# A four-layer graph stack on one core: the first feed-forward product as seven block products with streamed weights

## The chip, the cores and the metric

The kernel runs on one core of a Trainium2 chip, in one launch. The core has five engines with an instruction queue each: TensorE (PE in the profile, its weight loads PEld), VectorE (DVE), ScalarE (ACT), GpSimd (POOL) and SyncE (SP, which here issues every DMA). All data are 32-bit floats. The metric is the device time of a launch in microseconds (us); lower is better.

## The reference, cut to what matters

Four layers run one after the other over 128 graphs of 64 nodes with 512 features. Each adds its result to its input and normalizes the sum. Layer 0 is a linear neighbour sum, layer 1 a graph attention with four heads, an output attention and a feed-forward part, and layers 2 and 3 are plain graph attentions. The feed-forward part of layer 1 is what the change is about:

```python
h = jax.nn.elu(_gat_heads(enc_inputs, adj, W_heads, a_heads))
h = jnp.transpose(h, (0, 2, 1, 3)).reshape(B, N, -1)
out = _gat_heads(h, adj, W_out[None], a_out[None])[:, 0]
out = jax.nn.elu(out)
ffn = jnp.maximum(out @ w1 + b1, 0.0) @ w2 + b2
y = ffn + out
```

Here `w1` and `w2` are 512 x 512, and `out` has 512 features for each node.

## The kernel before, in words

**Tiling.** The 8192 nodes are cut into 32 pairs of tiles, T = 2 tiles of P = 128 nodes each. Every pair goes through stages, each a Python generator: `stage_first` (layer 0), `stage_scores` (the heads' attention), `stage_heads`, `stage_project` (the product with W_out), `stage_out` (output attention, feed-forward, norm) and `stage_gat` for layers 2 and 3. Several pairs are under way at once, in different stages. The last pair takes another way from the output attention on: `stage_last` loads whole weights, and `stage_tile` does each of its two tiles by itself with plain products.

**Seven products.** A product of two matrices, each cut into 2 x 2 blocks, can be had from seven block products instead of eight, with additional sums of blocks before and after (the Strassen-Winograd form). `seven` (L633) is the frame for this: it takes two PSUM tiles, `stx_...` and `sty_...`, issues product 0 to 6 with a pause of `gap` between them, and adds the results into the four blocks of the output. With `fresh` the first write of a block is a copy on ScalarE (four of them), and three adds on VectorE follow. `once` is the hook for a subtraction that must come after the first product, `whole` the hook for what follows when half of the output is ready. No more than UNITS = 3 such units are under way together.

There are two uses of it. `strassen` (L685) keeps the tokens stationary and moves the weights: a block product has `kc` matmuls with 256 moving columns. It serves layer 0, W_out, w2, W2 and W3. The heads (L1007) keep the weights stationary and move the tokens, so that their result comes out transposed: a block product is 2 x 2 matmuls with 128 moving columns.

**Weights.** `stage_stream` (L580) runs once for each streamed weight near the start: it loads the four blocks, stores three of them to DRAM as they are, forms four differences on GpSimd and stores these too. `part_from` (L613) later loads one of the seven parts for one product. For weights of 512 rows a part is 256 KB and lies in the ring `wk` of six buffers, which w2, W2 and W3 share; the ring `ws` of four buffers is for parts of 512 KB.

**The first feed-forward product**, in `stage_out` (L1112 to L1127), is not of this kind. `w1` is loaded once (L562) and stays on chip, 8 KB on each partition. For each pair it makes the tile `hid`, transposed, from the transposed input `oT`: two PSUM tiles `hidp`, each with two groups of four matmuls of 256 moving columns, and a Relu with the bias on ScalarE out of PSUM for each group. `oT` and `hid`, like the tiles `gT` of layers 2 and 3, are of the tag "A", of which there are NA = 2 buffers. After `hid` come its sums and the product with w2, whose tiles are named `y_...`.

**Order.** No instruction is issued where it is written. The class `Plan` records every operation as a step with a rank, its place in the recording, and `order` (L229) then simulates the five queues with a rough cost for each step (`cost`, L353) and issues on each engine what is ready with the lowest rank. `WAIT` and `SLACK` are the delays that it supposes between engines, `NEAR` is how far a step may run ahead for a free buffer, and the table `LATER` shifts the rank of steps by kind: "te:hidp/S" stands for TensorE steps that write hidp in the first 11% of all steps, "/E" for those in the last 7%. All DMAs are issued by SP in the order that comes out of this, and each waits there for its buffer. In the profile nearly everything has the line L336, where steps are played, so that tiles are told apart by name.

Of the kernel before, what the change touches and what calls it, by code (L numbers as in the profile page):

```python
# [12 lines left out]
FP = mybir.dt.float32  # L13
BF = mybir.dt.bfloat16
I32 = mybir.dt.int32
AF = mybir.ActivationFunctionType
# [21 lines left out]

WAIT = 0.152
NEAR = 150
SLACK = {"tensor": 0.8, "sync": 0.4}

LATER = {
    "gp:never/S": -100, "gp:rs_i": -60, "gp:s_o/S": -20, "gp:ys/E": -40, "sc:aT": -100,
    "sc:aTg/S": 20, "sc:elu/S": -40, "sc:hT": 120, "sc:oT": 60, "sc:who": -80, "sc:xT": -200,  # L50
    "sc:xT/S": -180, "sc:ys/S": 132, "sy:beta/S": -12, "sy:raw_w": 180, "te:fp/S": -20,
    "te:hidp/E": -40, "te:hidp/S": 28, "te:l": 29, "te:l/S": 69, "te:pt": -28, "te:pt/E": 200,
    "ve:e": -29, "ve:e/S": 40, "ve:f_o/S": -120, "ve:hT": 100, "ve:has": 200, "ve:mv": -100,
    "ve:mv/E": 100, "ve:mx": -20, "ve:o": -140, "ve:r": -40, "ve:r/E": 40, "ve:sh": 10,
    "ve:sm": -80, "ve:st": -13,
}


# [315 lines left out]
def gnn_stack_kernel(  # L374
# [45 lines left out]
        nc.sync.dma_start(out=t, in_=x[ts(p, T * P), :].rearrange("(t p) d -> p t d", p=P))  # L420
        return t

    def weight(src, rows, name):
        t = wp.tile([P, rows // P, D], FP, tag=name, name=name)
        nc.sync.dma_start(out=t, in_=src.rearrange("(c p) o -> p c o", p=P))
        return t
# [282 lines left out]
    def sums(A, kc, eng):  # L709


        def make(name):
            s2, s3 = (
                unit.tile([P, kc, P], FP, tag=f"s{i}", bufs=2, name=f"s{i}_{name}")
                for i in (2, 3)
            )
            eng.tensor_tensor(s2, A(0, 1), A(0, 0), ALU.subtract)
            eng.tensor_tensor(s3, A(1, 1), s2, ALU.subtract)
            return (
                A(0, 1), s2, s3,  # L720
                lambda a: eng.tensor_tensor(a, a, s2, ALU.subtract),
            )
        return make


    def moments(x, name):
# [280 lines left out]
    def stage_heads():  # L1007

        for i in range(NP * H):
            p, h = divmod(i, H)  # L1010
            while p not in ys:
                yield 1.0
            y, t1, t2 = ys[p][h // 2]
            y, t1, t2 = y[:, :, h % 2, :, :], t1[:, :, h % 2, :], t2[:, :, h % 2, :]
            Y = lambda k, t: y[:, 2 * k : 2 * k + 2, t, :]
            w = w_h[h]
            hT = unit.tile([P, KC, T, P], FP, tag="hT", bufs=H, name=f"hT_{p}_{h}")

            def product(i, ps, first, last):
                a = w[:, :, (2, 0, 1, 4, 6, 5, 3)[i], :]  # L1020
                b = (Y(1, 0), Y(0, 0), t1, t2, Y(1, 1), Y(0, 1), Y(1, 0))[i]
                with nc.together():
                    for c in range(2):
                        for k in range(2):
                            nc.tensor.matmul(
                                ps[:, c, :], lhsT=a[:, k, ts(c, P)], rhs=b[:, k, :],
                                start=(first and c == 0 and k == 0),
                                stop=(last and c == 1 and k == 1), skip_group_check=True,
                            )

            def t4():
                nc.gpsimd.tensor_tensor(Y(1, 0), Y(1, 0), t2, ALU.subtract)

            yield from seven(
                product, lambda i, j: hT[:, 2 * i : 2 * i + 2, j, :], [2, P], f"h_{p}_{h}",
                TURN / H / 8 * haste(p), True,
                t4,
                lambda i: elu_of(hT[:, 2 * i : 2 * i + 2, :, :], f"{p}_{h}_{i}"),
            )
            hTs[p, h] = hT  # L1040
            if h == H - 1:
                ys.pop(p)
# [41 lines left out]
    def stage_out(p):  # L1084
# [19 lines left out]
        for t in range(T):  # L1104
            ps = psum.tile([P, KC, P], FP, tag="b", name=f"oTp_{p}_{t}")
            with nc.together():
                for k in range(KC):
                    nc.tensor.transpose(ps[:, k, :], o[:, t, ts(k, P)], ident)
            nc.scalar.copy(oT[:, :, ts(t, P)], ps)
            nc.gpsimd.tensor_tensor(o[:, t, :], o[:, t, :], b2_sb, ALU.add)  # L1110
            yield 2.0
        hid = unit.tile([P, 2, T, KC // 2, P], FP, tag="A", bufs=NA, name=f"hid_{p}")  # L1112
        for q in range(KC // 2):
            ps = psum.tile([P, 2, T * P], FP, tag="b", name=f"hidp_{p}_{q}")
            for c in range(2):
                with nc.together():
                    for k in range(KC):
                        nc.tensor.matmul(
                            ps[:, c, :], lhsT=w1_sb[:, k, ts(2 * q + c, P)], rhs=oT[:, k, :],
                            start=(k == 0), stop=(k == KC - 1),  # L1120
                        )
            for c in range(2):
# [69 lines left out]
    def stage_last(p):  # L1192

        raw = {}
        for name, src, tag, bufs in (("w2", w2, "ax", 1), ("W2", W2, "ys", 2), ("W3", W3, "ys", 2)):
            raw[name] = unit.tile([P, KC, D], FP, tag=tag, bufs=bufs, name=f"{name}_last")
            nc.sync.dma_start(out=raw[name], in_=src.rearrange("(c p) o -> p c o", p=P))
        r = unit.tile([P, 2, D], FP, tag="hT", bufs=H, name="rows_last")
        for i, src in enumerate((b2, gamma)):
            nc.sync.dma_start(out=r[:, i, :], in_=src.partition_broadcast(P))  # L1200
        who, aT = yield from out_attention(p)
        o = xp.tile([P, T, D], FP, tag="x", name=f"o_{p}")
        shared.update(raw=raw, rows=r, who=who, aT=aT, o=o)
        yield 2.0
        for name in ("2", "3"):
            shared[name] = rows([score[name][s, :] for s in range(2)], f"{name}_{p}")
            yield 2.0

    def stage_tile(p, t):
# [33 lines left out]
        for c in range(KC):  # L1243
            with nc.together():
                for k in range(KC):
                    nc.tensor.matmul(
                        ps[:, c, :], lhsT=w1_sb[:, k, ts(c, P)], rhs=oT[:, k, :],
                        start=(k == 0), stop=(k == KC - 1),
                    )
        for c in range(KC):  # L1250
# [52 lines left out]
    def start(at, order, stage):  # L1303
        heapq.heappush(queue, (at, order, stage))
# [88 lines left out]
```

## Time and profile before

| what | value |
|---|---|
| time, median of 3 runs | 3308.72 us (3306.71 to 3319.2) |
| the profiled execution | 3313.95 us |
| its span on the core | 3312.2 us |
| mean granted TensorE clock | 0.994 of full speed |
| matmul records of hidp in 31 pairs | 992, of 256 columns |
| matmul records of hidp in the last pair | 64, of 128 columns |
| DMA traffic | 726.08 MB, mean 219 GB/s |
| DMA instructions issued by SP | 2086 |

The span runs from the first to the last instruction of the program, and the launch around it makes up the rest of the execution's time. In a row of a group the columns are line, engine, operation, output<-inputs, shape and count, then busy time in us and mean ns of one, then the idle time before them and what ended it. The mean ns of one matmul is longer than its share of the engine, since matmuls overlap. Records whose operands differ have rows of their own.

First and last weight-stationary run of the hidden layer in stage_out: the first starts at 197.7 us, the last at 3205.9.

### The profile page before, as it was taken

The page shows a single profiled execution, that of the slowest core. Times are in us where ns is not written, and L with a number is a line of the kernel's source. Part 1 is how long each engine was busy: PE and PEld are TensorE (multiplying, and loading weights), DVE is VectorE, ACT ScalarE, POOL GpSimd, SP SyncE. Part 2 cuts the span into 40 slices and gives each one's busy share as a digit, 9 for nine tenths or more (in the row PEclk, how much of TensorE's full clock was granted, in tenths as well). Part 3 has the DMA queues.
Part 4 walks back from the last instruction along what each step waited for, and adds up shares of the span by engine and source line. Part 5 has one row for each costly group of instructions (what it writes and reads, how often), then busy time and mean ns, then how long its engine had stood idle before and what let it go on. Part 6 is the DMA issues. An engine that isn't in the chain of part 4 may idle for free.

```text
span 3312.2 us, 60000 instructions
## 1 busy us (share of the span) xinstructions
PE 3265.2 (99%) x21268; PEld 2881.8 (87%) x21268; DVE 2374.4 (72%) x5668; ACT 1364.6 (41%) x3226; POOL 1724.0 (52%) x1860
## 2 busy tenths in 40 slices
PE   8999999999999999999999999999999999999997
PEld 4888888898988989989889988888889899898885
DVE  5467767777777777777777777777777767777766
ACT  2434344343444434444443443434444344343442
POOL 6745445554555555455454555645554455554442
PEclk9999999999999999999999999999999999999998
DMA  8956666767667676667766667676666766667652
GB/s 303 338 177 215 221 203 215 234 208 237 211 210 233 213 247 197 200 230 221 242 204 220 212 217 236 214 226 208 214 233 208 246 201 202 229 216 238 227 183 77
DMA packets 306584, 726.08 MB, mean 219 GB/s; under 512 B 34240, under 2 KB 43504, under 8 KB 306288
## 3 DMA queue, kind: packets, MB, share of 16 engines
q1 hardware_dynamic: 306288, 722.26, 67.1%
q8 instruction: 171, 2.80, 0.3%
q14 instruction: 125, 1.02, 0.1%
HBM read 688.69 MB, written 33.44 MB: 218 GB/s over the span
## 4 chain that ended last, share of the span: by engine, by line
PE 91%; DVE 4%; DMA 3%; POOL 1%; issue 1%; ACT 0%; SPq 0%; POOLq 0%; DVEq 0%; ACTq 0%
PE stx_h L336 13%; PE stx_o L336 13%; PE stx L336 12%; PE sty_h L336 10%; PE sty_o L336 9%; PE sty L336 9%; PE hidp L336 7%; PE yp L336 4%; PE gp L336 3%; PE stx_y L336 3%; PE sty_y L336 2%; PE axp L336 2%; PE l L336 1%; PE op L336 1%; PE oTp L336 1%; DMA d_f<-f 1%
## 5 line engine op out<-in xcount | busy, mean ns | idle before, releaser
L336 DVE CUSTOM_DVE_ANT_0 j<-x,rows 128x512 bf16<-128x512 f32 x736 | 584.1, 794 | 94.3 <-DMA rows<-d_h 75.6
L336 PE MATMUL stx_h<-ys,wh 128*128 128x128 f32 x3072 | 403.8, 275 | 0.7 <-DVE hT L336 0.7
L336 PEld LDWEIGHTS stx_h<-ys,wh 128*128 128x128 f32 x3072 | 381.1, 192 | 22.3 <-DVE sh L336 5.7
L336 POOL TENSOR_SCALAR rs<-mv 128x1 f32<-128x1 f32 x256 | 104.1, 407 | 406.2 <-DVE mv L336 392.2
L336 ACT COPY hT<-stx_h 128x256 f32<-128x256 f32 x384 | 143.0, 372 | 384.6 <-PE stx_h L336 378.6
L336 ACT ACTIVATE x<-x,sh,rs 128x512 f32<-128x512 f32 x256 | 207.2, 813 | 223.6 <-DVE sh L336 221.0
L336 PE MATMUL sty_h<-ys,wh 128*128 128x128 f32 x2048 | 273.8, 277 | 0.0
L336 PEld LDWEIGHTS sty_h<-ys,wh 128*128 128x128 f32 x2048 | 254.4, 192 | 9.0 <-issue 0.5
L336 PE MATMUL stx_o<-ws_wo_T,s_o 128*128 128x256 f32 x1024 | 246.0, 383 | 0.5 <-ACT who L336 0.5
L336 DVE TENSOR_TENSOR x<-stx,x 128x256 f32<-128x256 f32 x360 | 150.8, 420 | 132.1 <-PE stx L336 131.0
L336 PE MATMUL sty_o<-ws_wo,hT 128*128 128x256 f32 x1024 | 243.2, 380 | 0.1
L336 PE MATMUL hidp<-oT,w 128*128 128x256 f32 (+1 forms) x1056 | 228.9, 373 | 0.0
L336 PEld LDWEIGHTS hidp<-oT,w 128*128 128x128 f32 x1056 | 194.0, 190 | 24.9 <-ACT oT L336 0.2
L336 PEld LDWEIGHTS stx_o<-ws_wo_T,s_o 128*128 128x128 f32 x1024 | 190.2, 191 | 28.4 <-ACT who L336 2.1
L336 PEld LDWEIGHTS sty_o<-ws_wo,hT 128*128 128x128 f32 x1024 | 190.8, 191 | 25.6 <-issue 1.1
L336 DVE SCALAR_TENSOR_TENSOR hT<-elu,hT 128x512 f32<-128x512 f32 x256 | 174.9, 684 | 43.3 <-ACT elu L336 41.3
L336 POOL TENSOR_TENSOR ys<-ys,t 128x256 f32<-128x256 f32 x128 | 102.9, 814 | 189.8 <-PE sty_h L336 189.4
L336 ACT ACTIVATE elu<-hT 128x512 f32<-128x512 f32 x256 | 153.0, 599 | 108.7 <-DVE hT L336 104.6
L336 POOL TENSOR_TENSOR rs<-rs,mhalf 128x1 f32<-128x1 f32 x256 | 173.4, 677 | 21.1
L336 DVE BATCH_NORM_STATS2 st<-x 128x6 f32<-128x512 f32 x256 | 176.5, 689 | 5.1
L336 DVE TENSOR_TENSOR hT<-sty_h,hT 128x256 f32<-128x256 f32 x256 | 107.2, 420 | 81.2 <-PE sty_h L336 69.3
L336 ACT COPY ys<-yp 128x512 f32<-128x512 f32 x256 | 132.2, 602 | 78.4 <-PE yp L336 71.7
(205 smaller groups left out, 7629.3 us busy)
## 6 DMA issues: line engine op xcount, KB each, us to landing
ws_wo_T<-d_wo_T SPq DMA_DIRECT2D x256, 512.0 KB, 3.9
ws_wo<-d_wo SPq DMA_DIRECT2D x192, 512.0 KB, 5.3
ws_W_T<-d_W_T SPq DMA_DIRECT2D x248, 256.0 KB, 4.2
rows<-d_h SPq DMA_DIRECT2D x240, 256.0 KB, 4.7
ws_w_T<-d_w_T SPq DMA_DIRECT2D x112, 512.0 KB, 4.9
ws_W<-d_W SPq DMA_DIRECT2D x186, 256.0 KB, 4.1
ws_w<-d_w SPq DMA_DIRECT2D x84, 512.0 KB, 5.2
rows<-d SPq DMA_DIRECT2D x128, 256.0 KB, 4.3
```

Of the source, the lines that this page charges most:

```text
L336: getattr(getattr(self.tc.nc, s.engine), name)(*map(real, args), **{k: real(v) for k, v in kw.items()})
```

## The change

The product with w1 is done by seven block products, as the heads do it: weights stationary, tokens moving.

- `left` is what was inside `stage_heads`, taken out as a helper for both. A product is four weight tiles of 128 x 128, each against 128 moving columns.
- `stage_stream` gets a form `left=True` with the block sums for this orientation (one of the four is a sum). It is run for w1 just before w2, and the seven parts of w1 are loaded for each pair through the ring `wk`.
- In `stage_out` three differences of blocks of `oT` are made on GpSimd (t1, t2 in the tags s2 and s3 of two buffers, and one in place), a fourth inside the product. The Relu with its bias is done in place on `hid` in SBUF, half of it when each half of the rows is whole.
- The whole w1 on chip goes. The last pair loads it at the end as two tiles of the tag "hT".
- NA is 3 instead of 2: the tag "A" has a third buffer of 4 KB on each partition.
- `WAIT`, `NEAR`, `SLACK` and the whole table `LATER` have other values. All entries of the table are replaced; most kinds of steps now have one.

```diff
-NA = 2
+NA = 3
...
-WAIT = 0.152
-NEAR = 150
-SLACK = {"tensor": 0.8, "sync": 0.4}
+WAIT = 0.2
+NEAR = 177
+SLACK = {"tensor": 0.786, "sync": 0.744}
...
 LATER = {
...
-    "te:hidp/E": -40, "te:hidp/S": 28, "te:l": 29, "te:l/S": 69, "te:pt": -28, "te:pt/E": 200,
...
+    "te:axp/S": -3, "te:bc": -22, "te:bc/S": -13, "te:bc_o": -2, "te:bc_o/E": -16, "te:fp": -58,
...
-    w1_sb = weight(w1, D, "w1")
...
-    def stage_stream(src, name):
+    def stage_stream(src, name, left=False):
...
         for out, a, b, place in (
+            ("S1", "12", "22", "12"), ("S2", "S1", "11", "11"), ("S3", "22", "S2", "22"),
+            ("S4", "21", "S2", "21"),
+        ) if left else (
             ("T1", "12", "11", "11"), ("T3", "22", "12", "12"), ("T2", "22", "T1", "22"),
             ("T4", "21", "T2", "21"),
         ):
             parts[out] = parts[place]
-            nc.gpsimd.tensor_tensor(parts[out], parts[a], parts[b], ALU.subtract)
+            op = ALU.add if out == "S1" else ALU.subtract
+            nc.gpsimd.tensor_tensor(parts[out], parts[a], parts[b], op)
             store(out)
...
+    def left(A, Y, t1, t2, R, name, gap, whole):
...
+        def product(i, ps, first, last):
+            a = A(i)
+            b = (Y(1, 0), Y(0, 0), t1, t2, Y(1, 1), Y(0, 1), Y(1, 0))[i]
+            with nc.together():
+                for c in range(2):
+                    for k in range(2):
+                        nc.tensor.matmul(
+                            ps[:, c, :], lhsT=a[:, k, ts(c, P)], rhs=b[:, k, :],
+                            start=(first and c == 0 and k == 0),
+                            stop=(last and c == 1 and k == 1), skip_group_check=True,
+                        )
+
+        yield from seven(
+            product, R, [2, P], name, gap, True,
+            lambda: nc.gpsimd.tensor_tensor(Y(1, 0), Y(1, 0), t2, ALU.subtract), whole,
+        )
...
-        oT = unit.tile([P, KC, T * P], FP, tag="A", bufs=NA, name=f"oT_{p}")
+        oT = unit.tile([P, KC, T, P], FP, tag="A", bufs=NA, name=f"oT_{p}")
...
+        O = lambda k, t: oT[:, 2 * k : 2 * k + 2, t, :]
+        t1, t2 = (
+            unit.tile([P, 2, P], FP, tag=f"s{i}", bufs=2, name=f"t{i}_o_{p}") for i in (2, 3)
+        )
+        nc.gpsimd.tensor_tensor(t1, O(0, 1), O(0, 0), ALU.subtract)
+        nc.gpsimd.tensor_tensor(t2, O(1, 1), t1, ALU.subtract)
+        nc.gpsimd.tensor_tensor(O(0, 1), O(1, 1), O(0, 1), ALU.subtract)
         hid = unit.tile([P, 2, T, KC // 2, P], FP, tag="A", bufs=NA, name=f"hid_{p}")
-        for q in range(KC // 2):
-            ps = psum.tile([P, 2, T * P], FP, tag="b", name=f"hidp_{p}_{q}")
+
+        def relu(q):
             for c in range(2):
...
+                h = hid[:, q, :, c, :]
                 nc.scalar.activation(
-                    hid[:, q, :, c, :], ps[:, c, :].rearrange("p (t i) -> p t i", t=T), AF.Relu,
-                    bias=b1_sb[:, 2 * q + c : 2 * q + c + 1],
+                    h, h, AF.Relu, bias=b1_sb[:, 2 * q + c : 2 * q + c + 1]
                 )
-            yield 6.0
+
+        part = part_from("w1", p, D // 2)
+        yield from left(
+            lambda i: part(("21", "11", "S1", "S2", "S4", "S3", "22")[i]), O, t1, t2,
+            lambda i, j: hid[:, i, j, :, :], f"1_{p}", 1.8, relu,
+        )
+        yield 2.0
...
+            w = unit.tile([P, KC // 2, D], FP, tag="hT", bufs=H, name=f"w1_last_{i}")
...
-    start(0.2 * TURN, 0, stage_stream(w2, "w2"))
+    start(0.2 * TURN, 0, stage_stream(w1, "w1", True))
+    start(0.25 * TURN, 0, stage_stream(w2, "w2"))
```

More of the change, by code (lines that the diff above doesn't have):

```diff
@@ L32 @@
 AHEAD = 4
-WAIT = 0.152
-NEAR = 150
-SLACK = {"tensor": 0.8, "sync": 0.4}
+WAIT = 0.2
+NEAR = 177
+SLACK = {"tensor": 0.786, "sync": 0.744}
 LATER = {
-    "gp:never/S": -100, "gp:rs_i": -60, "gp:s_o/S": -20, "gp:ys/E": -40, "sc:aT": -100,
-    "sc:aTg/S": 20, "sc:elu/S": -40, "sc:hT": 120, "sc:oT": 60, "sc:who": -80, "sc:xT": -200,
-    "sc:xT/S": -180, "sc:ys/S": 132, "sy:beta/S": -12, "sy:raw_w": 180, "te:fp/S": -20,
-    "te:hidp/E": -40, "te:hidp/S": 28, "te:l": 29, "te:l/S": 69, "te:pt": -28, "te:pt/E": 200,
-    "ve:e": -29, "ve:e/S": 40, "ve:f_o/S": -120, "ve:hT": 100, "ve:has": 200, "ve:mv": -100,
-    "ve:mv/E": 100, "ve:mx": -20, "ve:o": -140, "ve:r": -40, "ve:r/E": 40, "ve:sh": 10,
-    "ve:sm": -80, "ve:st": -13,
+    "gp:aT": 74, "gp:aTg": -57, "gp:ax": 265, "gp:bones": 37, "gp:bones/S": -4, "gp:fill": 355,
+    "gp:fill/S": 18, "gp:gT": -122, "gp:gT/E": 149, "gp:gT/S": 190, "gp:hT": 12,
+    "gp:hT/E": -128, "gp:hT/S": -11, "gp:hid": 120, "gp:hid/E": -135, "gp:hid/S": -74,
+    "gp:ident": -132, "gp:ident/S": -6, "gp:mhalf": -131, "gp:never": 123, "gp:never/S": -154,
+    "gp:o": 151, "gp:o/E": -32, "gp:o/S": -53, "gp:oT/S": -67, "gp:raw_W/S": 91, "gp:raw_w": 5,
+    "gp:raw_w/S": 13, "gp:raw_wo": 1, "gp:raw_wo/S": -67, "gp:rs": 6, "gp:rs/E": 23,
+    "gp:rs/S": 10, "gp:rs_i": -4, "gp:rs_i/E": 101, "gp:rs_i/S": -21, "gp:s/S": 82,
+    "gp:s_o": -45, "gp:s_o/E": 17, "gp:s_y": 86, "gp:s_y/E": -69, "gp:s_y/S": 27, "gp:t/E": -5,
+    "gp:t_o/S": -89, "gp:wh/S": 32, "gp:x": -164, "gp:x/E": -26, "gp:x/S": 32, "gp:ys": 6,
+    "gp:ys/E": 162, "gp:ys/S": 32, "sc:a": 88, "sc:a/S": -25, "sc:aT": 23, "sc:aT/E": 87,
+    "sc:aT/S": -6, "sc:aT_o": 36, "sc:aTg": -32, "sc:aTg/E": -114, "sc:aTg/S": -189,
+    "sc:a_h": -164, "sc:a_h/S": 54, "sc:ax": -80, "sc:ax/S": -88, "sc:bc": 42, "sc:bc/S": -2,
+    "sc:elu": -63, "sc:elu/S": 36, "sc:f": 269, "sc:f/E": -42, "sc:f/S": 84, "sc:gT": 28,
+    "sc:gT/E": -203, "sc:gT/S": 46, "sc:hT/E": 1, "sc:hT/S": 41, "sc:hid": -40, "sc:o": -310,
+    "sc:o/E": -10, "sc:o/S": 189, "sc:oT": 67, "sc:oT/E": 26, "sc:oT/S": -75, "sc:sm": -33,
+    "sc:sm/E": 28, "sc:sm/S": -66, "sc:sm_o": -265, "sc:sm_o/E": -57, "sc:wat": 7,
+    "sc:wat/S": -202, "sc:wat_h": 68, "sc:who/E": -28, "sc:x/E": 35, "sc:x/S": -7, "sc:xT": 113,
+    "sc:xT/S": -7, "sc:ys": 190, "sc:ys/E": 132, "sc:ys/S": -87, "sy:W_last": -205,
+    "sy:W_last/E": -99, "sy:adj_i/S": -35, "sy:b_sb": -44, "sy:b_sb/S": 17, "sy:beta": 87,
+    "sy:beta/S": -52, "sy:d": 230, "sy:d/S": -92, "sy:d_W": 155, "sy:d_W/S": 24, "sy:d_W_T": 25,
+    "sy:d_W_T/S": 9, "sy:d_f": 63, "sy:d_f/S": 59, "sy:d_h": 195, "sy:d_h/S": 71, "sy:d_w": 134,
+    "sy:d_w/S": 96, "sy:d_w_S": 27, "sy:d_w_S/S": -201, "sy:d_w_T/S": -39, "sy:d_wo": 22,
+    "sy:d_wo/S": 41, "sy:d_wo_T/S": -120, "sy:dram": -347, "sy:dram/E": 51, "sy:dram/S": -195,
+    "sy:over/S": -95, "sy:raw_W": -19, "sy:raw_W/S": 18, "sy:raw_w": -17, "sy:raw_w/S": 27,
+    "sy:raw_wo": 85, "sy:raw_wo/S": -159, "sy:rows": 37, "sy:rows/E": 45, "sy:rows/S": -250,
+    "sy:rows_a/S": -1, "sy:rows_b/E": 160, "sy:rows_b/S": -82, "sy:rows_gamma": -64,
+    "sy:rows_gamma/E": 5, "sy:rows_gamma/S": -48, "sy:rows_last/E": 112, "sy:rows_o": -211,
+    "sy:rows_o/E": 183, "sy:rows_o/S": 39, "sy:w/S": -4, "sy:w_last": 108, "sy:w_last/E": 33,
+    "sy:wh": 29, "sy:ws_W": -76, "sy:ws_W/E": -96, "sy:ws_W_T": 44, "sy:ws_W_T/E": 53,
+    "sy:ws_w/E": -43, "sy:ws_w/S": -90, "sy:ws_w_S": 43, "sy:ws_w_S/E": 51, "sy:ws_w_T": -136,
+    "sy:ws_w_T/E": 1, "sy:ws_w_T/S": -23, "sy:ws_wo": -88, "sy:ws_wo/E": -293,
+    "sy:ws_wo_T": 143, "sy:ws_wo_T/S": -34, "sy:x": -14, "te:abd_ps/S": -7, "te:axp": -2,
+    "te:axp/S": -3, "te:bc": -22, "te:bc/S": -13, "te:bc_o": -2, "te:bc_o/E": -16, "te:fp": -58,
+    "te:fp/E": -35, "te:fp/S": 2, "te:gp/E": -16, "te:l": 40, "te:oTp/E": 41, "te:oTp/S": 3,
+    "te:op/E": -49, "te:op/S": 31, "te:pt": -41, "te:pt/E": -59, "te:pt_o": -14,
+    "te:pt_o/E": 78, "te:stx/E": -29, "te:stx_h/S": -1, "te:stx_y": -6, "te:stx_y/E": -47,
+    "te:stx_y/S": 5, "te:sty/S": -116, "te:sty_y/S": 37, "te:wap": -66, "te:wap/S": -61,
+    "te:wap_h": 361, "te:wap_h/S": -130, "te:xTp": -56, "te:xTp/S": 36, "te:yp/E": 73,
+    "te:z": -82, "te:z/E": -277, "ve:adj_f": 208, "ve:adj_f/S": -107, "ve:aggr": 4,
+    "ve:aggr/S": -49, "ve:bc/E": -74, "ve:bc/S": -72, "ve:deg": 175, "ve:degb/S": -56,
+    "ve:e": -42, "ve:e/E": -48, "ve:e/S": 64, "ve:e_o": -61, "ve:f/E": -19, "ve:f_o": 125,
+    "ve:f_o/E": -7, "ve:gT": 6, "ve:gT/E": -35, "ve:hT": -6, "ve:hT/E": -54, "ve:hT/S": -21,
+    "ve:has": -89, "ve:has/S": -4, "ve:hid": -116, "ve:hid/S": 281, "ve:ident": -47,
+    "ve:ident/S": 141, "ve:mv/E": -45, "ve:mv/S": -26, "ve:mv_i": -135, "ve:mv_i/E": -38,
+    "ve:mv_i/S": -108, "ve:mx": 28, "ve:mx/E": 63, "ve:mx/S": -21, "ve:ng": 39, "ve:ng/E": 7,
+    "ve:ng/S": 66, "ve:nm": 21, "ve:nm/E": 41, "ve:nm/S": -3, "ve:nm_o": 46, "ve:nm_o/E": -107,
+    "ve:o": -125, "ve:o/S": -13, "ve:over/S": -50, "ve:r": 59, "ve:r/E": 115, "ve:r/S": -7,
+    "ve:r_o": -214, "ve:r_o/E": 163, "ve:r_o/S": 81, "ve:sh/E": -65, "ve:sm": 31,
+    "ve:sm/E": -67, "ve:sm/S": -13, "ve:some": -40, "ve:some/S": -43, "ve:st/S": -15,
+    "ve:st_i": 293, "ve:st_i/E": -79, "ve:st_i/S": 66, "ve:wa": 22, "ve:wa/S": 24,
+    "ve:wa_h/S": -30, "ve:who": -5, "ve:who/E": -167, "ve:x": 16, "ve:x/E": -55, "ve:x/S": 128,
@@ L421, in load_x @@
         return t
[L423 to L426, printed above, removed]
     def row(src, name):
@@ L1017, in stage_heads @@
             hT = unit.tile([P, KC, T, P], FP, tag="hT", bufs=H, name=f"hT_{p}_{h}")
[L1019 to L1037, printed above, removed]
+            yield from left(
+                lambda i: w[:, :, (2, 0, 1, 4, 6, 5, 3)[i], :], Y, t1, t2,
+                lambda i, j: hT[:, 2 * i : 2 * i + 2, j, :], f"h_{p}_{h}",
+                TURN / H / 8 * haste(p),
                 lambda i: elu_of(hT[:, 2 * i : 2 * i + 2, :, :], f"{p}_{h}_{i}"),
@@ L1108, in stage_out @@
                     nc.tensor.transpose(ps[:, k, :], o[:, t, ts(k, P)], ident)
-            nc.scalar.copy(oT[:, :, ts(t, P)], ps)
+            nc.scalar.copy(oT[:, :, t, :], ps)
             nc.gpsimd.tensor_tensor(o[:, t, :], o[:, t, :], b2_sb, ALU.add)
             yield 2.0
+        O = lambda k, t: oT[:, 2 * k : 2 * k + 2, t, :]
[5 more added lines that the diff above has]
+        nc.gpsimd.tensor_tensor(O(0, 1), O(1, 1), O(0, 1), ALU.subtract)
         hid = unit.tile([P, 2, T, KC // 2, P], FP, tag="A", bufs=NA, name=f"hid_{p}")
-        for q in range(KC // 2):
-            ps = psum.tile([P, 2, T * P], FP, tag="b", name=f"hidp_{p}_{q}")
+        def relu(q):
             for c in range(2):
[L1116 to L1122, printed above, removed]
+                h = hid[:, q, :, c, :]
                 nc.scalar.activation(
-                    hid[:, q, :, c, :], ps[:, c, :].rearrange("p (t i) -> p t i", t=T), AF.Relu,
-                    bias=b1_sb[:, 2 * q + c : 2 * q + c + 1],
-                )
-            yield 6.0
+                    h, h, AF.Relu, bias=b1_sb[:, 2 * q + c : 2 * q + c + 1]
+                )
+        part = part_from("w1", p, D // 2)
+        yield from left(
+            lambda i: part(("21", "11", "S1", "S2", "S4", "S3", "22")[i]), O, t1, t2,
+            lambda i, j: hid[:, i, j, :, :], f"1_{p}", 1.8, relu,
+        )
+        yield 2.0
         gamma_sb = rows([gamma], f"gamma_{p}")[:, 0, :]
@@ L1197, in stage_last @@
             nc.sync.dma_start(out=raw[name], in_=src.rearrange("(c p) o -> p c o", p=P))
+        raw["w1"] = []
+        for i in range(2):
+            w = unit.tile([P, KC // 2, D], FP, tag="hT", bufs=H, name=f"w1_last_{i}")
+            nc.sync.dma_start(
+                out=w, in_=w1[ts(i, D // 2), :].rearrange("(c p) o -> p c o", p=P)
+            )
+            raw["w1"].append(w)
         r = unit.tile([P, 2, D], FP, tag="hT", bufs=H, name="rows_last")
@@ L1246, in stage_tile @@
                     nc.tensor.matmul(
-                        ps[:, c, :], lhsT=w1_sb[:, k, ts(c, P)], rhs=oT[:, k, :],
+                        ps[:, c, :], lhsT=raw["w1"][k // 2][:, k % 2, ts(c, P)], rhs=oT[:, k, :],
                         start=(k == 0), stop=(k == KC - 1),
```

## The prediction

> **What bounds the kernel now.** I read the page from the top: the busy shares, then the chain that ended last.
>
> ```profile
> span 3312.2 us, 60000 instructions
> ...
> PE 3265.2 (99%) x21268; PEld 2881.8 (87%) x21268; DVE 2374.4 (72%) x5668; ACT 1364.6 (41%) x3226; POOL 1724.0 (52%) x1860
> ...
> PE 91%; DVE 4%; DMA 3%; POOL 1%; issue 1%; ACT 0%; SPq 0%; POOLq 0%; DVEq 0%; ACTq 0%
> ```
>
> TensorE is busy for 99% of the span and holds 91% of the chain. A busy matmul row may hide waiting, because the ends are modelled. So I took the groups of TensorE by shape, and then a timeline from the middle of the run, where only the starts count.
>
> ```profile
> L336 PE MATMUL stx_h<-ys,wh 128*128 128x128 f32 x3072 | 403.8, 275 | 0.7 <-DVE hT L336 0.7
> L336 PE MATMUL hidp<-oT,w 128*128 128x256 f32 x992 | 221.6, 379 | 0.0
> ```
>
> ```profile
> 1060.53 1.03 PE L336 MATMUL sty<-ws_W,gT 128*128 128x256 f32 x4
> 1061.39 1.05 PE L336 MATMUL stx_h<-ys,wh 128*128 128x128 f32 x8
> 1062.28 1.03 PE L336 MATMUL stx<-ws_W_T,s 128*128 128x256 f32 x4
> ```
>
> From start to start, four records of 256 columns take 0.86 us and eight records of 128 columns 0.89 us: 216 ns and 112 ns each. (Every f32 matmul leaves two records: 16 matmuls x 31 pairs = 496, and the hidp row counts 992.) The switch between the two kinds costs nothing here, and the hidden layer's own long run keeps the same pace:
>
> ```profile
> 197.75 5.34 PE L336 MATMUL hidp<-oT,w 128*128 128x256 f32 x24
> 202.93 0.27 PE L336 MATMUL f2p<-ident,f 128*8 128x128 f32 x1
> ```
>
> 5.18 us for 24 records is 216 ns again. Now all records at such paces: 8748 of 256 columns x 0.216 = 1890; 8943 of 128 x 0.112 = 1002; 180 of 512 x 0.429 = 77; 3072 half-height ones, two side by side, x 0.056 = 172; 256 quarter tiles x 0.11 = 28. The sum is about 3169 us, so of 3312 about 143 us are lost by TensorE. Added up from the starts by fortieths of the span (83 us each), some 37 us of that lie in the first three, 31 in the last (its final wait included), and nearly all else is about 2 us in each of the others. TensorE's own work sets the time; a saving there counts nearly in full while the others keep up. The window over the middle millisecond shows their room:
>
> ```profile
> 1000.00:2000.00 1000.00, 999.07 (x6614) 895.29 (x6613) 736.72 (x1745) 420.65 (x994) 526.15 (x567) 1.00 0.68 219
> ```
>
> The columns are length, busy PE, PEld, DVE, ACT and POOL, the clock (full), DMA share and GB/s.
>
> **Step 1, TensorE.** Removed in each of 31 pairs: 32 records of 256 columns, 32 x 0.216 = 6.91 us. Added: seven products x 4 matmuls x 2 records of 128 columns, 56 x 0.112 = 6.27 us. The saving is 0.64 us a pair, **-20 us** in all. It is less than the eighth (0.86 us) that seven products for eight promise, because half the columns take 52% of the time. The last pair keeps its plain product.
>
> Two rules speak against this step. The Trainium skill, "TensorE: Matmul & The Clock Gate", section "Back-to-back issue gap", gives 56 ns for an isolated matmul of 128 columns, but 81 ns in a stream in which each has its own weight load. If a record is two passes (its formula has 109 ns for 256 columns, half of our 216), the stream figure makes 162 ns a record: 56 x 0.162 = 9.07 us against 6.91, so +67 us over 31 pairs. The row shows 112 ns in just such a stream, and it decides. "Perfetto Trace Analysis", section "Identifying the Most-Contended Engine", takes the busy share of weight loads as TensorE's measure. Loads for 128-column records are busy 381.1 / 3072 = 0.124 us each, for hidp 194.0 / 1056 = 0.184: 56 x 0.124 - 32 x 0.184 = +1.06 us a pair, +33 us if loads set the pace. Here matmuls of 128 columns start every 112 ns with a load for each, so loads do not add to that pace, but there is no slack under it either.
>
> **Step 2, new waits of TensorE.** The old product ran as one block after one copy, and its starts are 0.1 us late in total. The new one is seven groups, each behind a landed weight part, and four of them also behind a sum that POOL makes. I bound it by what there is: the t products of the heads lose nothing (0), and a whole weight load of 190 ns laid open at each of 217 groups would be 41 us. The nearest row is the second FFN product, seven groups in the same stage from the same ring; its starts are 9.7 us later than 216 ns apiece would have them. The heads' sevens lose 0.13 us each, which would be 4. I take **+8**, nearer to the FFN row.
>
> **Step 3, the other engines.** POOL: t1, t2, the difference and the late subtraction, each near the 869 ns of s_y, about 3.4 us a pair. In that millisecond, with some 9.5 pairs, 526 becomes about 558. DVE: three adds at 420 ns, 1.26 us a pair, 737 to 749. ACT: four copies at 372 ns come to the four Relus of 472, which stay, now in place: 421 to 435. All lie beside TensorE: 0. If that cover were gone, the longest new piece, POOL's three operations between the copies of oT and the sixth product (2.6 us x 31 = 80 us), would be laid open. Other pairs' groups stand in between, as for s_y now. DVE also loses pace beside POOL:
>
> ```profile
> L336 DVE CUSTOM_DVE_ANT_0 j<-x,rows 128x512 bf16<-128x512 f32 x736 | 584.1, 794 | 94.3 <-DMA rows<-d_h 75.6
> L336 DVE CUSTOM_DVE_ANT_0 j<-w,a 128x512 bf16<-128x512 f32 x16 | 10.9, 682 | 3.9 <-ACT a L336 3.6
> ```
>
> The same operation takes 112 ns more where both inputs are in SBUF. A tenth more of POOL's sums may add some 10 us to DVE's 2374; it has 25% free.
>
> **Step 4, DMA and SP's queue.** Seven parts of 256 KB in each of 31 pairs are 57 MB on 726, and DMA goes from 0.68 to about 0.73. SP issues 217 transfers more, at 0.32 us 69 us of a queue that idles most of the time. What matters is that each new transfer waits at SP's head for a buffer of the six in ring wk, with the loads of wo, W2, W3, score rows and b2 behind it. The ring serves 28 parts a pair instead of 21.
>
> ```profile
> ws_w_T<-d_w_T SPq DMA_DIRECT2D x124, 256.0 KB, 3.6
> ...
> ws_w<-d_w SPq DMA_DIRECT2D x93, 256.0 KB, 2.9
> ```
>
> A part lands 2.9 to 3.6 us after its issue. Six buffers at 28 parts per 105 us give 22 us of lead, 30 before. Products on the hidden layer waited for parts 7 times, 6.3 us, in the whole run. The same for the first product is inside step 2's +8.
>
> **Step 5, start and end.** The 1 MB load of w1 issued at 29 us goes, where DMA is busy 0.96 (up to 3 us gained at 330 GB/s). Later come 1 MB of blocks, 1.8 MB stored and four POOL operations of 1.27 us: 2.8 MB / 0.28 is 10 us of a DMA busy 0.8 before the first hidden layer at 197.5. From -3 to +10, I take **+1**: TensorE there waits mostly for attention steps. At the end w1 lands in two free hT buffers, with DMA at 0.3 to 0.5: 0.
>
> **Step 6, the buffer and the order.** oT and hid are now both held through seven products instead of 7 us. With two buffers that would shut out gT of W2 and W3; the third gives it back, 0. But the whole issue order is computed anew, with other constants and another table of shifts, and no row shows what it does to the 143 lost us. Twice the middle's 2 us per 83 us would be +70; half of all losses gone, -70. The table has entries for the first 11% and last 7% of steps, where some 68 of the lost us are. I take a tenth of the losses, **-14**.
>
> **Sum:** -20 + 8 + 0 + 1 - 14 = -25 us. Against the profiled execution (3313.95, span 3312.2) that is 3289; against the median 3308.72, which the profiled one exceeds by 5, it is **3284 us**, -0.75%. About 0.5%, 16.5 us, is what a measurement here can tell from no change.
>
> **Rivals.**
> (a) The gain is eaten: waits of step 2 and the order take back what the columns give. For it: step 1 is only 0.64 us a pair, and the lost time is a little everywhere. Steps 1 and 2 at -12, the start at +6 and no gain by order: **3303**.
> (b) The slower one: the ring and SP's queue. A w1 part waits at SP's head for a buffer which a W3 product of the pair before still holds; what is behind it is late too, and TensorE, in order, stands. For it: SP already waits 365.5 us, 233 times, for sty groups to free buffers. Against it: 22 us of lead for a landing of 3.6. Once a pair 2 us late is 62 us: 3308.7 - 25 + 62 = **3346**. It decides from 25 / 31 = 0.8 us a pair.
> (c) The 128-column stream falls to the page's 162 ns: 3284 + 87 = **3371**. The 7168 head records speak against it.
> (d) The new order does more than I grant, a third of the losses (-48 instead of -14): **3250**. The losses in the first and last stretches speak for it; that they are chains of dependent steps, against.
> That the change does not do what it says has no room: the counts follow from the loops.
>
> **How the numbers follow.** The forecast 0.52 (own range 3268 to 3298, by steps 2 and 5 and half of step 6), (a) 0.17, (b) 0.17, (c) 0.02, (d) 0.12. Faster by over 0.5% (below 3292): nine tenths of the forecast, all of (d) and a little of (a), 0.61. Within: the rest of the forecast, most of (a), a piece of (b), 0.21. Slower (above 3325): 0.18. The range from 3255 to 3342 leaves out the far parts of (d) and (b) and all of (c).
>
> **What would show it.** Right: a group of 1736 records of 128 columns in place of the 992, from start to start 112 ns; TensorE still 99% and near 22000 records; the first hidden layer begun no later than at 205 us. Step 2 is wrong if weight parts of w1 appear as what TensorE waits for, by over 20 us; step 3 if POOL's t does; step 4 if SP waits longer for sty and parts of wo land late; step 6 if the lost time in the middle is not near 2 us per 83. The prediction falls if the span shrinks by less than 9 us or TensorE's losses grow past 160.

## The result, and the profile after

The changed kernel takes **3379.67 us** (3378.1 to 3388.16, 4 runs) against 3309.69 before: ratio 1.0217 (1.0204 to 1.0229). It is 70 us slower, where 25 us less were forecast, and 38 us outside the range. The head of its page, and its chain:

```profile
span 3376.2 us, 62495 instructions
...
PE 3255.9 (96%) x22012; PEld 2884.5 (85%) x22012; DVE 2408.8 (71%) x5761; ACT 1407.6 (42%) x3350; POOL 1809.0 (54%) x1988
...
PE 82%; DMA 9%; DVE 4%; POOL 2%; issue 1%; SPq 1%; ACT 0%; POOLq 0%; DVEq 0%; ACTq 0%
```

TensorE has the 744 additional records that were forecast, and is busy for 9 us less. But it now stands still for 120 us of the span, 47 before, and the chain that ended last holds 82% of PE instead of 91, and 9% of DMA instead of 3. The window over the middle millisecond, with the columns of before (length, busy PE, PEld, DVE, ACT, POOL, clock, DMA share, GB/s), shows that this is so in the steady state:

```profile
1000.00:2000.00 1000.00, 982.99 (x6747) 884.64 (x6747) 739.95 (x1755) 422.95 (x1012) 544.62 (x595) 1.00 0.73 237
```

PE is at 983 instead of 999. The other engines have not become full: VectorE is at 740, GpSimd at 545, DMA at 0.73, near what was forecast for each. So none of them became the bound. What changed is who keeps TensorE waiting. From its view of waits in the changed kernel (engine and tile that waited, what released it, us in total, times, longest):

```profile
PE pt L380 <- DVE e L380: 16.0, 12, 5.7
...
PE sty L380 <- DMA ws_w<-d_w: 7.7, 5, 2.2
PE stx_y L380 <- DMA ws_w_T<-d_w_T: 5.5, 5, 1.8
PE sty L380 <- DMA ws_w_S<-d_w_S: 5.2, 4, 1.7
PE sty_y L380 <- DMA ws_w_T<-d_w_T: 5.0, 5, 1.8
```

And from the same view before:

```profile
PE pt L336 <- DVE e L336: 3.0, 4, 1.1
...
PE sty_y L336 <- DMA ws_w<-d_w: 1.3, 2, 0.9
```

All weight parts together made TensorE wait for 3.5 us before. Such idle time is only the visible part, since matmul ends are modelled. I therefore added up, for every record, how much later than its pace (216, 112, 429 ns and so on) the next one started, and put each delay of over 60 ns down to what released it (a few us could as well stand in another row, since the releasers are inferred):

| what TensorE was late for | before | after |
|---|---|---|
| results of VectorE | 37 us | 78 us |
| landed DMA parts | 12 us | 49 us |
| results of ScalarE | 25 us | 17 us |
| results of GpSimd | 2 us | 13 us |
| nothing that the profile shows | 85 us | 86 us |

The growth is 41 us for VectorE, 37 for landed parts, 11 for GpSimd, less 8 for ScalarE: 81. Less 21 us of saved columns that is 60 of the span's 64 us. The growth for landed parts is, in about equal halves of some 19 us, before the groups of w1 and before those of w2.

### The profile page after: what moved, and what is told of

It reads as the page before. It is cut to its first block, busy times and chain, and to the rows that moved or that the text cites. A ratio compares the mean times of both kernels' runs of the same rounds, so it can differ in the third digit from the quotient of the medians.

```text
span 3376.2 us, 62495 instructions
## 1 busy us (share of the span) xinstructions
PE 3255.9 (96%) x22012; PEld 2884.5 (85%) x22012; DVE 2408.8 (71%) x5761; ACT 1407.6 (42%) x3350; POOL 1809.0 (54%) x1988
## 4 chain that ended last, share of the span: by engine, by line
PE 82%; DMA 9%; DVE 4%; POOL 2%; issue 1%; SPq 1%; ACT 0%; POOLq 0%; DVEq 0%; ACTq 0%
PE stx L380 14%; PE stx_h L380 12%; PE stx_o L380 12%; PE sty L380 10%; PE sty_h L380 10%; PE sty_o L380 8%; PE yp L380 4%; PE gp L380 3%; PE stx_y L380 2%; PE sty_y L380 2%; DMA ws_w<-d_w 2%; PE axp L380 1%; DMA ws_w_T<-d_w_T 1%; PE op L380 1%; DMA rows<-d_h 1%
## 5 line engine op out<-in xcount | busy, mean ns | idle before, releaser
L380 DVE CUSTOM_DVE_ANT_0 j<-x,rows 128x512 bf16<-128x512 f32 x736 | 597.8, 812 | 66.0 <-DMA rows<-d_h 53.2
L380 POOL TENSOR_SCALAR rs<-mv 128x1 f32<-128x1 f32 x256 | 90.9, 355 | 408.2 <-DVE mv L380 388.5
L380 POOL TENSOR_TENSOR s<-gT 128x256 f32<-128x256 f32 x62 | 47.9, 772 | 199.8 <-DVE gT L380 177.0
L380 ACT ACTIVATE elu<-elu 128x512 f32<-128x512 f32 x256 | 149.0, 582 | 7.9
```

The source lines that it names most:

```text
L380: getattr(getattr(self.tc.nc, s.engine), name)(*map(real, args), **{k: real(v) for k, v in kw.items()})
```

## The experiments

All ratios are to runs of before on the same chip, with 95% intervals. "In place" means that the issue order of each engine is that of the kernel named, and only what is said differs.

**1. The saved columns alone (e5).** Before, in place, each hidp group of four matmuls of 256 columns played as seven of 128.

```diff
-                for name, args, kw in s.calls:
+                for name, args, kw in halves(s.calls):
```

`halves` cuts each call of such a group in two by columns and keeps four pieces for the first tile of tokens, three for the second.

> Before, with every instruction in its old place, but each group of four matmuls of 256 columns of hidp played as seven of 128 columns (four for the first tile of tokens, three for the second: the last quarter of the features of the second tile is left out). This is step 1 alone: 56 records of 128 columns for 32 of 256, no streaming, no other order. If the price of step 1 is right: 18 to 21 us faster than before, some 3288 us. If columns saved on TensorE are not time saved, because the next thing is late: 3300 to 3310 us. By the page's 162 ns a record: some 65 us slower.

Measured: 3286.82 us against 3307.8, ratio 0.9937 (0.9925 to 0.9949): **21 us faster**. In its timeline 56 records stand where 32 did:

```profile
1064.63 6.41 PE L357 MATMUL hidp<-oT,w 128*128 128x128 f32 x56
1070.88 1.89 PE L357 MATMUL stx_o<-ws_wo_T,s_o 128*128 128x256 f32 x8
```

6.25 us from start to start, 112 ns a record. Step 1's price is right, and in an undisturbed order all of it reaches the end. The 162 ns a record are an estimate, twice the 81 ns that the Trainium skill gives for a stream ("TensorE: Matmul & The Clock Gate", section "Back-to-back issue gap"); neither they nor the busy time of weight loads set the pace here.

**2. Product and order, crossed (e1, e2).** The new product and third buffer with the constants and table of before, and the old product with those of after. The edit is an exchange of `WAIT`, `NEAR`, `SLACK` and `LATER` between the two kernels.

> The new product and the third buffer, with the constants and the table of shifts of before. Theory O (the new order costs the time, not the product): 3285 to 3300 us, since step 1's 20 us are then there and the middle loses about 2 us per 83 us as before. Theory R (the ring wk and SP's queue make weight parts late): 3350 to 3390 us, with TensorE waiting for ws_w parts by some 30 us or more. Theory S (the seven groups of the new product themselves stall TensorE): also 3350 to 3390 us, with the losses at stx and sty groups that read oT.

> The old product with w1 on chip and two buffers, with the constants and the table of shifts of after. Theory O: as slow as after or more, 3370 to 3400 us (it has 20 us more of matmuls). Theories R and S: 3300 to 3330 us, near before, since the ring serves 21 parts a pair and the old product stands.

Measured: e1 3485.27 us, ratio 1.0542 (1.0521 to 1.0564); e2 3370.02 us, 1.0187 (1.0172 to 1.0202). Theory O had e2 right and e1 wrong by 190 us; R and S failed on e2, and no theory had e1, which is 95 us over their ranges too. With the old settings the new product costs 177 us, with the new ones (e2 to after) about 10. The new settings cost the old product 62 us and save the new one some 105. No part of the change has a price of its own: each pair of product and settings is another order.

**3. The two halves of the settings (e9 to e12).** Tables emptied, or constants exchanged alone.

```diff
-WAIT = 0.152
-NEAR = 150
-SLACK = {"tensor": 0.8, "sync": 0.4}
+WAIT = 0.2
+NEAR = 177
+SLACK = {"tensor": 0.786, "sync": 0.744}
```

> Before with an empty table of shifts: the planner's own order. Theory F (a table is fitted to one order of one structure, and the old product's table fits well while the new one's does not): 3360 us or more, and no better than the same with the new product. Theory O2 (the new table is bad by itself): near 3320 to 3340 us, well under the kernel with the old product and the new table (3370).

> After with an empty table of shifts. Theory F: 3390 to 3480 us, slower than after (its table does help its own structure). Theory O2: 3330 to 3365 us, faster than after. Against before with an empty table: if the new product itself is worth its 20 us once both are unfitted, this one is the faster of the two by 10 to 20 us; if streaming and seven waits eat it, slower by 10 to 40.

> Before with its own table but the new values of the supposed delays and of the look-ahead. Theory F: any move off the fitted point loses, 3325 to 3380 us. If the constants are harmless and the table is what costs in the kernel with the old product and the new order: 3300 to 3325 us.

> After with its table but the old values of the supposed delays and of the look-ahead. Theory F: slower than after, 3390 to 3450 us. If the new constants are what costs: 3310 to 3350 us.

Measured: e9 3333.51 us, 1.0065 (1.005 to 1.008); e10 3456.22 us, 1.0436 (1.0407 to 1.0465); e11 3370.29 us, 1.0177 (1.0162 to 1.0192); e12 3476.54 us, 1.0509 (1.0486 to 1.0532). For the old product the table is worth some 21 us and the constants decide: with the new ones it takes 3370 under either table. For the new product both are needed, by the ratios some 73 us for the table and 97 for the constants. "Any order but the fitted one is bad" (theory F) holds for the new product; for the old one it is too strong, since e9 came out under F's 3360, where O2 had put it. With both tables empty the new product is 123 us slower, not 10 to 40, though the constants of the two differ as well.

**4. How rough the ground is (e8).** Before with `WAIT` 0.155 for 0.152.

> Before, with one constant of the planner moved by a hair: the delay supposed between engines 0.155 us for 0.152. Same instructions, same buffers, but more than half of TensorE's stream comes out in another order. If a given order is one draw among many of about equal worth: 3300 to 3320 us. If the table of shifts was fitted to one exact order, so that any other loses: 3340 us or more. The second would mean that after, too, carries a loss which says nothing of the seven products.

Measured: 3324.45 us, 1.0048 (1.0035 to 1.0062). 17 us for three thousandths of a microsecond in a supposed delay, between the two expectations. This is nearly as large as the whole gain of step 1. By the names in the two traces, 29% of the places in TensorE's stream hold another record than in before (with all new constants, e11, it is 55%). Pairs share their names, so this is the least that has moved; the "more than half" of the expectation is not shown.

**5. What streaming costs in after's order (e6, e7, e3, e4).** e6 is after in place, without the loads of w1's parts from the second pair on (`kept` names these tiles). e7 is after in place, with eight buffers in ring `wk` on the chip and an order still made for six. In e3 and e4 the order is made for eight as well, with after's settings and with before's.

```diff
+                if s.engine == "sync" and any(kept(t) for t in s.uses):
+                    continue
...
+            if args["tag"] == "wk":
+                args["bufs"] = REAL_WK
...
-NWK = 6
+NWK = 8
```

(The first two lines are e6's, the next two e7's, the last two those of e3 and e4.)

> After, with every instruction in its place, except that the parts of w1 are not loaded from the second pair on: all seven products read one part that stays on chip (one block of w1 stands for all seven parts from the second pair on). So ring wk serves 21 parts a pair again and 57 MB of traffic go. If streaming w1 is the whole cause: 3290 to 3310 us. If it is the late weight parts only, beside a new order that costs by itself: 3335 to 3355 us, with TensorE's waits for landed parts down from some 49 us to 10 or 20, and the waits for VectorE's results as before it. If the order is all: 3370 to 3380.

> After, with every instruction in its place, but ring wk has eight buffers on the chip while the order is still computed for six. Only the waits for a free buffer become shorter. If the six buffers make the parts late: 20 to 40 us faster than after, 3340 to 3360 us. If SP's order, with transfers standing behind others that wait, is what makes them late, or if they are not what matters: 3365 to 3385 us.

> After, with eight buffers in the ring wk instead of six, nothing else. Theory R: a good part of the 70 us comes back, 3320 to 3345 us, and the DMA waits of TensorE (some 32 us of idle time before groups that read ws_w parts) fall to a few us. Theory O: 3365 to 3390 us, since the order is what it is; at most the 32 us of those waits can go. Theory S: no change.

> The first of these kernels with eight buffers in the ring wk. Theory O: within 10 us of the first. Theory R: 30 us or more faster than the first. Theory S: no change against the first.

Measured: e6 3361.7 us, 1.0157 (1.0139 to 1.0175), some 18 us under after and between two of the expectations; lateness for landed parts falls from 49 to 24 us, that for VectorE stays at 76. e7 3373.73 us, 1.0203 (1.0188 to 1.0219), not to be told from after, with lateness for landed parts some 3 us less. e3 3411.48 us, 1.0307 (1.0288 to 1.0326), slower than after; e4 3428.94 us, 1.037 (1.0342 to 1.0398), 56 us faster than e1. Theory R is half right: in after's order weight parts are late because of the streaming, but not for want of buffers on the chip. With before's settings e4 has some 31 us of this lateness and e1 some 80, so there eight buffers help; whether by the buffers or by the order that was made for them is not shown. One of these waits in after, first on TensorE:

```profile
2344.69 1.03 PE L380 MATMUL stx<-ws_W_T,s 128*128 128x256 f32 x4
2347.83 1.13 PE L380 MATMUL sty<-oT,ws_w 128*128 128x128 f32 x8 [2.12 <-DMA ws_w<-d_w]
2348.79 1.47 PE L380 MATMUL stx<-oT,ws_w 128*128 128x128 f32 x8
```

The first group of the new product stands 2.12 us for its part. SP's queue just before that:

```profile
2335.05 0.32 SPq L380 DMA_DIRECT2D ws_wo_T<-d_wo_T  x1
2338.79 1.41 SPq L380 DMA_DIRECT2D rows<-d_h  x2
2340.30 0.38 SPq L380 DMA_DIRECT2D rows_gamma<-in_gamma_dram  x1
2340.77 0.38 SPq L380 DMA_DIRECT2D ws_wo_T<-d_wo_T  x1
2341.25 0.38 SPq L380 DMA_DIRECT2D ws_W_T<-d_W_T  x1
2341.68 0.96 SPq L380 DMA_DIRECT2D ws_w<-d_w  x2
2344.02 2.05 SPq L380 DMA_DIRECT2D ws_w_S<-d_w_S  x3
```

SP issued nothing for 3.4 us, and then five transfers, 1.5 MB, one right after the other, before w1's first part. In the waits of SP for this stretch the longest single one names the engine and tile it stood for (first line). The second line is from GpSimd's timeline:

```profile
SPq L380 <- POOL o L380: 3.0, 1, 3.0
...
2335.82 2.95 POOL L380 TENSOR_TENSOR o<-o,rows_b 128x512 f32<-128x512 f32 x2 [6.23 <-DMA rows_b<-in_b_dram]
```

GpSimd's sum on o frees a buffer of `rows` (the one with b2, for which it had stood itself), not one of `wk`; the two score rows at SP's head waited for it, and the w1 parts stood behind them. The part issued at 2341.68 let TensorE go at 2347.8, some 6 us later, where a part took 2.9 to 3.6 before. In these 6 us the DMA engines were full (share 1.01, 327 GB/s), with the burst and with the w1 parts that followed at once:

```profile
2341.70:2347.80 6.10, 4.01 (x23) 3.26 (x22) 5.31 (x15) 1.55 (x3) 1.42 (x2) 1.00 1.01 327
```

A second wait, at 2042.29, shows the same sequence; the other late groups were not followed up. SP's stand behind GpSimd's sum is nothing new. In the whole run, before and after:

```profile
SPq L336 <- POOL o L336: 57.5, 20, 5.3
...
SPq L380 <- POOL o L380: 34.6, 16, 4.5
```

New is that w1's parts, which TensorE needs soon after, stand behind it as well. With eight buffers on the chip (e7) the same group of the same pair stands as long:

```profile
2340.28 1.13 PE L384 MATMUL sty<-oT,ws_w 128*128 128x128 f32 x8 [2.07 <-DMA ws_w<-d_w]
```

**6. The side work (e13).** e6, and in place without the new product's three adds on VectorE and four sums on GpSimd.

```diff
+                if s.kind in ("gp:t_o", "ve:hid", "gp:oT"):
+                    continue
```

> After with every remaining instruction in its place, but besides the loads of w1's parts (one kept part stands for all from the second pair on) also the new product's work on the other engines is left out: its three adds on VectorE and its four sums on GpSimd (the products read blocks of oT as they are). If the direct costs of streaming and side work are the cause of the 70 us: 3290 to 3310 us. If it is the order in which TensorE's work now stands, which remains: 3335 to 3360 us, with TensorE's waits for VectorE hardly fewer than in after.

Measured: 3347.2 us, 1.0122 (1.0103 to 1.014), in the range expected if TensorE's order is what costs, and far from the other. By the ratios, the side work costs some 12 us on top of the streaming. TensorE's waits in this kernel:

```profile
PE pt L398 <- DVE e L398: 18.4, 15, 5.7
PE bc L398 <- DVE f L398: 9.3, 5, 2.6
PE bc L398 <- DVE over L398: 8.3, 1, 8.3
PE stx_y L398 <- DMA ws_w_T<-d_w_T: 5.4, 5, 2.0
```

The lateness for VectorE is 71 us, little under after's 78, although nothing of the new product runs on VectorE or GpSimd any more. So it isn't the adds that make pt and bc wait. That their matmuls stand too near behind VectorE's steps in this order is the reading that is left, and the old product with the same settings (e2) has the same wait:

```profile
PE pt L380 <- DVE e L380: 17.7, 8, 6.3
```

**7. Other orders (e14 to e18).** Settings changed step by step, keeping a step when the planner's own reckoning came out no later, for the new product with eight and with six buffers and for the old one. All edits are of this kind, here e16 (the table is other than that of after throughout):

```diff
-WAIT = 0.2
-NEAR = 177
-SLACK = {"tensor": 0.786, "sync": 0.744}
+WAIT = 0.152
+NEAR = 212
+SLACK = {"tensor": 0.683, "sync": 0.23}
...
```

> The new product with eight buffers in ring wk and an order fitted afresh: constants and table moved step by step, each step kept when the planner's own reckoning of the end came out no later. If the new product as such is sound, and after's loss is a poor order under a ring of six: faster than before, 3270 to 3300 us. If seven groups, streaming and the side work cost TensorE whatever the order: 3330 us or more.

> Before, with an order fitted afresh in the same way and for as long. It tells how much of the gain of the kernel with the new product and eight buffers would be had from fitting alone: if the new product carries it, this one stays at 3290 to 3310 us, 15 us or more behind; if fitting carries it, the two are within 10 us.

> After with six buffers as it is; only the constants and the table of shifts are others, fitted from the table of before. If after's loss is its order: well below after's 3380, at 3310 to 3350 us, with less TensorE waiting in the middle. If the six buffers hold the new product back in any order: 3360 us or more.

> The new product with eight buffers in ring wk, the order of e14 fitted further, now also against slower landings of transfers. e14 lost some 15 us at the start and the end and had only 2 to 3 us per 83 us in the middle. If that can be mended by order: 3295 to 3315 us, level with before or faster. If the start with w1's added stream and the denser DMA keep their price: 3320 to 3340 us.

> The control of the other two: the old product, fitted further in the same way. 3290 to 3315 us; the old product keeps its place if the best of the new ones stays over it.

Measured: e14 3332.2 us, 1.0076 (1.0057 to 1.0094); e15 3308.1 us, 0.9996 (0.9986 to 1.0005); e16 3377.14 us, 1.0207 (1.0192 to 1.0222); e17 3342.15 us, 1.0105 (1.0088 to 1.0122); e18 3319.93 us, 1.0039 (1.0024 to 1.0055). With eight buffers and another order the new product comes 47 us nearer, but no order that was tried takes it below before. With six buffers, e16 ends where after ended, in the range for "the six buffers hold it back", and has the same 49 us for landed parts; in e14 they are 24 us and in e17 27. One order doesn't show that of every order, and the searches behind e14 and e16 were not the same, so that the buffers' share in the 47 us is open. e18 missed its range, and both orders that were fitted further ended 10 to 14 us later by the ratios than those they came from (e17 than e14, e18 than e15): the planner's own reckoning does not see differences of this size.

None of the complete kernels beats before (e15 is level with it); e5 does, but leaves work out.

## Why the prediction was wrong

- **What bounds the kernel:** right for before. That "a saving there counts nearly in full while the others keep up" held where the order stood (e5). Whether the others keep up depends on the order: the same instructions lose 17 us more with `WAIT` at 0.155 (e8).
- **Step 1 (-20):** right, -21 (e5). The choice of the row against the two rules was right, though e5, which leaves out an eighth of the product's work, has none of the new waits.
- **Step 2 (+8):** too small. "Nearer to the FFN row" took the waits of the second product in an order made for it. Lateness for landed parts alone grew by 37 us, about half of it before the w1 groups, half before those of w2, which share the ring.
- **Step 3 (0):** the busy times were right, and the engines did not fill. The cost was still some 12 us in after's order (e6 to e13), where "all lie beside TensorE" was said; with intervals of about 6 us on either side its size is rough.
- **Step 4 (inside step 2):** the wrong thing was counted. In the waits followed up, six buffers and 22 us of lead did not protect a part, because its issue stood behind other transfers in SP's queue. Rival (b) had this mechanism and its sign; its 62 us were too much for it alone. With streaming left out 18 come back (e6). Its blocker also was another one: in the wait shown above a buffer of `rows`, not one held by W3; and two more buffers in the ring brought nothing in this order (e7).
- **Step 5 (+1):** too small, though not settled in size. Its sign held: the first hidden layer began at 195.6 us, before at 197.7. But in the 50 us from 50 on TensorE ran 192 records, 260 before, with DMA at 0.93 instead of 0.80 and a granted clock of 0.90 instead of 0.97. Over the first 250 us its lateness is 39 us in after, 32 before, and 36 in e2, so about half of this belongs to the new settings.
- **Step 6 (-14): the step that failed.** "I take a tenth of the losses" gave the new order a gain. With the old product the same settings cost 62 us (e2), and the constants alone do as much (e11), and with the new product they save 105 against before's. The bound of +70 had been worked out in that step, and the middle's loss did near double; the value was taken at the wrong end without a row for it, and the range stopped short of it. A supposed delay of 0.2 us was read as one more number of the change, where a far smaller move of it already puts other records into over a quarter of TensorE's places (e8).

The path from before to after is then, in order: new settings with the old product +62 (e2), and the new product and its buffer on top +10. In that +10 are the saved 21 us, streaming and side work of some 30 (e6, e13), and what the further shift of the order adds; only the sum is measured in one step. Run the other way round, the product comes first at +177 and the settings give back 105. What stays open: whether an order exists in which the new product pays. The ten complete kernels with it, in nine orders, lie between 3332 and 3485 us, the seven with the old product between 3308 and 3370. The third buffer was not tried by itself, so that its share in the +177 and the +10 is open.

## What to carry to other kernels

Where one engine is full and its program is interleaved by a planner, a change of the program is a change of the whole order. Price the operations if you like, but give the order a range of its own, from what other settings do to the unchanged kernel: here between nothing (e15) and 62 us lost, against 21 to be won. To find out what an operation is worth, take it out in place, with every other instruction where it was.

A buffer ring's lead says little when its loads share one in-order queue with others: ask what can stand at the head of that queue, and what will be issued in a burst when it goes.

## What the runs showed of the hardware

Matmuls of 128 columns with a fresh 128x128 weight tile each ran at 112 ns a record, in runs of 56 records and in groups of eight alike: half a 256-column record plus 4 ns, although their weight loads are busy for 115 (e5) to 124 ns each (the heads) by the profile. A part of 256 KB, 2.9 to 3.6 us from issue to landing in the median of before, let TensorE go only about 6 us after its issue behind a burst of five transfers (1.5 MB), with DMA full in just these 6 us and at 0.73 in the mean of the middle millisecond.

VectorE's score sums `j<-x,rows`, with both inputs in SBUF, took 686 ns in the mean of before where no two-input operation of GpSimd ran beside them (441 of them), and 990 ns where such operations ran for more than half of their time (228). With an input in PSUM (`j<-w,a`) the same operation took 684 ns in such company (9). In after 284 of the 736 stand in it. What this is worth in time is not shown.
